# A graph attention layer: the softmax scans of both directions side by side, one feature tile per edge group

## The chip, the core and the metric

The kernel runs on one core of a Trainium2 chip. The metric is the time of one execution on the device in microseconds. Three runs of the kernel before took 5300.75, 5307.96 and 5309.53 us; their median, 5307.96 us, is the time before.

In the profile the engines are PE (TensorE's matmuls), PEld (TensorE's weight loads), DVE (VectorE), ACT (ScalarE), POOL (GpSimd) and SP (SyncE). A q behind a name is the engine's sequencer. L167 is line 167 of the kernel.

## What is computed

There are 12500 nodes with 64 features, and 400000 edges with 64 features each. The edges are sorted by their destination.

```python
h_src, h_dst = x[src], x[dst]
e = leaky_relu(concat([h_src, h_dst, edge]) @ W_attn + b_attn, 0.01)[:, 0]
m = concat([h_src, edge]) @ W_ne
ex = exp(e - segment_max(e, dst)[dst])
alpha = ex / segment_sum(ex, dst)[dst]
z = segment_sum(alpha[:, None] * m, dst)
out = relu(concat([x, z]) @ W_out)
return layernorm(x + out)
```

So each edge gets a score, a softmax runs over all edges of one destination, and the edges' features are summed with its weights. Since a destination's edges are neighbours in the list, the softmax is over runs of the list. It is made with scans along the list in both directions.

## The kernel before

A **group** is 512 edges: 128 partitions with 4 edges each. There are 782 groups. A **batch** is up to 20 groups, and its softmax is one piece of work; the batches are 4 groups, then 38 of 20, then 10 and 8. A **feature tile** is 4 groups (`SG`), so a batch of 20 has five.

`gather` (L152) fills a feature tile. It holds two arrays, `ze` with the edges' own rows and `zx` with 65 values for the edge's source node: its features and its share of the score. SyncE loads `ze` with one transfer of 512 KB (L158). GpSimd gathers `zx` with 16 indirect transfers, one per group and place (L167), from `table`, which the kernel makes itself first; the first batch gathers from `x` (`plain`), one tile of it before anything else. The pool has ten such tiles (`ZB`). A gather waits for the last product of the batch that owned the tile ten tiles earlier (L172); with five tiles to a batch this is the batch before last.

`scores` (L178) is VectorE's work per tile: a product with `w_edge` and a reduction (L190, L192), the gathered share (L197), a 0/1 array `hot` that tells which of 48 destination slots an edge belongs to (L199), the destination's share by that array (L204, L207), and the leaky ReLU (L208, L209). ScalarE copies the window of destination values `win` to PSUM (L186), from a row that SyncE loads (`wrow`, L184).

`softmax` (L252) turns a batch's scores into one long list. Its 80 groups of 128 edges (four per group) lie one per partition, 128 edges along the row (`er`, L279). A scan over the whole list is made in three steps: a scan within each partition, a scan over the 128 partial results in one row of one partition, and a second scan within the partitions from the right start. `to_row` (L212) brings the partial results into a row: a 32x32 block transpose and four copies of 32 values, each from another group of 32 partitions (L218). `to_col` (L226) goes back: four copies into `turn` (L228) and a transpose (L223). The maximum needs such a pass forwards (L283 to L293), then one backwards over its result (`total`, L295 to L306); after the exponential (L313) the sum again needs one forwards (L314 to L327) and one backwards. So four passes follow one another, and all their steps but two are VectorE's. `carry` hands the running maximum and sum to the next batch; `fac` corrects what an open run has in the accumulator already (L337 to L344).

`aggregate` (L347) makes `w`, the weights by slot, on VectorE (L350). TensorE multiplies, for each group and place, 128 edges by 48 slots: one product for the edges' own rows into partitions 0 to 63 of the result and one for the gathered rows into 64 to 127 (L358). VectorE adds each group's 48 columns to the accumulator `acc` in SBUF at a place read from memory (L368).

The main loop (L546 on) takes for each batch `gather` and `scores` tile by tile, then `softmax`, then `aggregate`. A scheduler orders the instructions of each engine from this program and its own model of time, and each engine works in that order; there is one queue per engine, and the transfers that an engine issues stand in it too. `finish1` and `finish2` (L482, L499) turn finished blocks of nodes into output, two calls at most per batch, beside the other work. `neighbours` (L231) loads the destinations with those before and behind.

## Time and profile before

| | us |
|---|---|
| median of three runs | 5307.96 |
| the profiled execution | 5279.3 |
| its span, first to last instruction | 5277.6 |
| POOL busy | 2978.4 |
| DVE busy | 2211.2 |
| PE busy | 657.6 |
| ACT busy | 245.8 |

A row of the costliest groups names line, engine, operation and tiles, then the count, the busy time in us, the mean of one in ns, and after the bar the engine's idle time just before these instructions with what ended most of it. "issue" there is time in which the engine waited for nothing that the profile shows. A row of the timeline starts with the time since the start and the duration in us, and has the idle time before it in brackets. A row of the chain of waits has start, duration, and what it was; x64 is the number of records in it.

The clock granted to TensorE was 0.57 of full speed on average: half speed, and full speed for some 7 to 14 us in each batch's products. The transfers moved 47 GB/s on average.

### The profile page before, as it was taken

The numbers are of one execution on the slowest core, as the hardware profiler recorded it, in microseconds if no ns is written. First come the engines' busy times: TensorE is split into PE (matmuls) and PEld (weight loads), VectorE is DVE, ScalarE is ACT, GpSimd is POOL, SyncE is SP. The second block draws the span as 40 slices with busy tenths as digits, with TensorE's granted clock in tenths as the row PEclk, the third lists the DMA queues.
The fourth block names the chain that finished last, engine by engine and source line by source line (L and its number), as shares of the span: only waits on it lengthen the run. The fifth ranks groups of instructions, "written<-read, shape, count | busy, mean of one in ns | idle before, by whom it ended". The sixth has DMA issues, their size and how long they took to land.

```text
span 5277.6 us, 40966 instructions
## 1 busy us (share of the span) xinstructions
PE 657.6 (12%) x13346; PEld 612.9 (12%) x13346; DVE 2211.2 (42%) x6612; ACT 245.8 (5%) x527; POOL 2978.4 (56%) x3142
## 2 busy tenths in 40 slices
PE   0010000000100111101011111111111111111113
PEld 0010000000100010101010110110111111111112
DVE  4163343344444444444444444444444444444446
ACT  0000000000000000000000000000000000000001
POOL 4745555556555555555555555555555555555550
PEclk9985555555555555555555555555555555555556
DMA  7111111122211121111111211211221222221110
GB/s 133 28 48 46 45 45 45 45 46 47 47 46 46 46 48 46 47 46 47 46 47 45 48 47 46 48 47 46 47 48 47 47 47 47 47 47 46 46 43 10
DMA packets 304921, 249.29 MB, mean 47 GB/s; under 512 B 125445, under 2 KB 253869, under 8 KB 304698
## 3 DMA queue, kind: packets, MB, share of 16 engines
q0 software_dynamic: 100320, 104.46, 10.7%
q1 hardware_dynamic: 177690, 135.46, 9.0%
q10 hardware_dynamic: 26688, 6.67, 0.6%
q8 instruction: 107, 1.75, 0.1%
q14 instruction: 116, 0.95, 0.1%
HBM read 239.69 MB, written 9.07 MB: 47 GB/s over the span
## 4 chain that ended last, share of the span: by engine, by line
issue 58%; DVE 26%; PE 7%; another core or an unknown queue 4%; DMA 2%; POOL 1%; DVEq 1%; SPq 1%; ACT 0%; ACTq 0%
PE pg L358 5%; DVE prod L190 2%; DVE hot L199 2%; DVE acc L368 2%; DVE row L218 2%; DVE turn L228 1%; DVE sdst L207 1%; DVE y L192 1%; DVE tr L215 1%; DVE prod L204 1%; POOL zx L167 1%; PE pg L505 1%; PE pg L504 1%; DMA zx<-table,srcs 1%
## 5 line engine op out<-in xcount | busy, mean ns | idle before, releaser
L167 POOL DMA_INDIRECT zx<-table,srcs x3112 | 2948.1, 947 | 2109.0 <-PE pg L358 1140.7
L358 PE MATMUL pg<-w,ze 128*64 128x48 f32 x6256 | 476.5, 249 | 3669.8 <-DVE w L350 2103.7
L358 PEld LDWEIGHTS pg<-w,ze 128*64 128x64 f32 x6256 | 468.6, 167 | 3674.9 <-DVE w L350 2007.4
L218 DVE COPY row<-tr 1x32 f32<-1x32 f32 x656 | 137.5, 210 | 847.2 <-issue 671.5
L358 PE MATMUL pg<-w,zx 128*64 128x48 f32 x6256 | 477.5, 249 | 25.7 <-issue 25.7
L358 PEld LDWEIGHTS pg<-w,zx 128*64 128x64 f32 x6256 | 468.3, 167 | 28.8 <-issue 28.8
L192 DVE TENSOR_REDUCE y<-prod 128x16 f32<-128x1024 f32 x196 | 237.4, 1211 | 3.2 <-remote 3.2
L190 DVE TENSOR_TENSOR prod<-ze,fixed 128x1024 f32<-128x1024 f32 x196 | 237.2, 1210 | 0.0
L207 DVE TENSOR_REDUCE sdst<-prod 128x16 f32<-128x768 f32 x196 | 185.4, 946 | 19.9 <-DVE drel L142 14.5
L204 DVE TENSOR_TENSOR prod<-hot,win 128x768 f32<-128x768 bf16 x196 | 186.1, 950 | 11.8 <-DVE y L197 10.7
L368 DVE TENSOR_TENSOR acc<-acc,pg 128x48 f32 x782 | 153.9, 197 | 88.3 <-PE pg L358 84.7
L199 DVE TENSOR_TENSOR hot<-fixed,drel 128x768 bf16<-128x768 f32 x196 | 185.8, 948 | 0.0
L350 DVE TENSOR_TENSOR w<-hot,fixed 128x768 f32<-128x768 bf16 x196 | 175.9, 947 | 1.2
L228 DVE COPY turn<-rt_m 1x32 f32<-1x32 f32 x164 | 34.0, 208 | 235.2 <-issue 211.1
L131 PE MATMUL pp<-ident,nat 20*128 20x20 f32 (+3 forms) x328 | 42.6, 269 | 716.3 <-DVE sdst L207 241.0
L131 PEld LDWEIGHTS pp<-ident,nat 20*128 20x128 f32 (+3 forms) x328 | 39.0, 197 | 723.4 <-issue 703.8
L186 ACT ACTIVATE win<-wrow 128x192 f32<-128x192 f32 x196 | 65.0, 331 | 1152.8 <-DVE prod L204 798.9
L134 DVE CAST srcs<-pp 128x80 int32<-128x80 f32 (+3 forms) x41 | 9.8, 238 | 249.4 <-DMA zx<-table,srcs 246.5
L228 DVE COPY turn<-top 1x32 f32<-1x32 f32 x164 | 33.6, 205 | 169.9 <-issue 168.5
L228 DVE COPY turn<-den 1x32 f32<-1x32 f32 x164 | 31.9, 194 | 157.2 <-issue 155.7
L323 ACT ACTIVATE drop<-drop 1x1 f32<-1x1 f32 x40 | 8.1, 202 | 1793.4 <-DVE b_m L306 1088.5
L505 PE MATMUL pg<-both,acc 128*128 128x64 f32 x196 | 64.4, 430 | 97.7 <-DVE acc L368 82.1
(129 smaller groups left out, 1267.9 us busy)
## 6 DMA issues: line engine op xcount, KB each, us to landing
ze<-in_edge_dram SPq DMA_DIRECT2D x194, 512.0 KB
zx<-table,srcs POOLq DMA_INDIRECT x3112
wrow<-wins SPq DMA_DIRECT2D x195, 96.0 KB
table<-xt ACTq DMA_DIRECT2D x14, 227.5 KB
xb<-in_x_dram ACTq DMA_DIRECT2D x24, 128.0 KB
out_dram<-yo SPq DMA_DIRECT2D x24, 128.0 KB
raw<-in_idx_dram SPq DMA_DIRECT2D x38, 80.0 KB
xt<-in_x_dram SPq DMA_DIRECT2D x13, 224.0 KB
```

Of the source, the lines that this page charges most:

```text
L167: got = nc.gpsimd.indirect_dma_start(out=zx[:, g, t, 0:D] if plain else zx[:, g, t, :], out_offset=None, in_=x[:, :] if plain else table[: ...
L190: nc.vector.tensor_tensor(prod[:, 0:n], ze[:, 0:n], w_edge.unsqueeze(1).to_broadcast([P, n, T, D]), op=OP.mult)
L192: nc.vector.tensor_reduce(yb, prod[:, 0:n], axis=AX.X, op=OP.add)
L199: nc.vector.tensor_tensor(hot[:, 0:n], slots.unsqueeze(1).unsqueeze(1).to_broadcast([P, n, T, S]), drel[:, :, b:b + n].rearrange("p t g -> ...
L204: nc.vector.tensor_tensor(at[:, 0:n], hot[:, 0:n], win[:, 0:n].unsqueeze(2).to_broadcast([P, n, T, S]), op=OP.mult)
L207: nc.vector.tensor_reduce(sdst[:, 0:n], at[:, 0:n], axis=AX.X, op=OP.add)
L218: nc.vector.tensor_copy(row.rearrange("o (g h) -> o h g", h=HQ)[:, h, :], tr[h * BG:h * BG + 1, :])
L228: nc.vector.tensor_copy(turn[h * BG:h * BG + 1, :], row.rearrange("o (g h) -> o h g", h=HQ)[:, h, :])
L350: nc.vector.tensor_tensor(w[:, 0:n], hot[:, 0:n], alpha[:, :, b:b + n].rearrange("p t g -> p g t").unsqueeze(3).to_broadcast([P, n, T, S]) ...
L358: last = nc.tensor.matmul(pg[at:at + D, g, :], z[:, g, t, 0:D], w[:, g, t, :], start=(t == 0), stop=(t == T - 1))
L368: added = nc.vector.tensor_tensor(ag, ag, pg[:, g, :], op=OP.add)
L505: nc.tensor.matmul(po[:, j, :], acc[:, (c0 + j) * P:(c0 + j + 1) * P], both, start=False, stop=True)
```

## The change

- The softmax's forward and backward scans no longer follow one another. Both start from the scores (later from the exponentials), lie side by side in one tile `pair`, and go through one row and back together (`to_rows`, `to_cols`). The maximum is the larger of both; the sum is both minus the edge's own value, which both hold. The correction factor of a batch's first run goes back with them as a third row of `srow`.
- A feature tile is one array `z` of 129 values per edge: 64 edge values, and the 65 gathered ones behind them. SyncE loads the edges' rows into one of two staging tiles `ze`, ScalarE copies them into `z`, and GpSimd gathers into the rest. There are nine such tiles. 
- TensorE makes one product of 128 columns per 128 edges, where it made two of 64.
- The first two batches, of 4 and 20 groups, become one of 24. All its six tiles are gathered from `x` ahead of the rest of the start.

The diff, without changed arguments of calls:

```diff
@@ -29,7 +29,9 @@
-ZB = 10
+ZB = 9
+ZW = 129
+EB = 2
@@ -151,8 +153,8 @@
     def gather(g0, n, srcs, b0, plain):
-        ze = feats.tile([P, SG, T, D], F32, name="ze")
-        zx = feats.tile([P, SG, T, EW], F32, name="zx")
+        z = feats.tile([P, SG, T, ZW], F32, name="z")
+        ze = chunks.tile([P, SG, T, D], F32, name="ze", bufs=EB)
         whole = min(n, NG - 1 - g0)
         if whole:
             nc.sync.dma_start(out=ze[:, 0:whole].rearrange("p g t f -> p g (t f)"),
@@ -161,11 +163,12 @@
             nc.vector.memset(ze[:, n - 1], 0.0)
             nc.sync.dma_start(out=ze[0:RP, n - 1],
                               in_=edge[E - REST:E, :].rearrange("(p t) f -> p t f", t=T))
+        nc.scalar.activation(z[:, 0:n, :, 0:D], ze[:, 0:n], AF.Copy)
         for g in range(n):
             for t in range(T):
                 at = srcs[:, t, g0 + g - b0:g0 + g - b0 + 1]
                 got = nc.gpsimd.indirect_dma_start(
-                    out=zx[:, g, t, 0:D] if plain else zx[:, g, t, :], out_offset=None,
+                    out=z[:, g, t, D:2 * D] if plain else z[:, g, t, D:ZW], out_offset=None,
                     in_=x[:, :] if plain else table[:, :],
                     in_offset=bass.IndirectOffsetOnAxis(ap=at, axis=0))
                 if len(owner) >= ZB:
@@ -209,24 +212,23 @@
         nc.vector.scalar_tensor_tensor(yb, sdst[:, 0:n], SLOPE, sdst[:, 0:n], op0=OP.mult, op1=OP.max)
         return hot
-    def to_row(block):
-
-        tr = rows.tile([P, BG], F32, name="tr")
-        nc.vector.transpose(tr, block)
-        row = tiny.tile([1, P], F32, name="row", bufs=1)
+    def to_rows(pair):
+
+        tr = rows.tile([P, 2, BG], F32, name="tr")
+        nc.vector.transpose(tr, pair[:, :, 0:BG])
+        row = tiny.tile([1, 2, P], F32, name="row", bufs=1)
         for h in range(HQ):
-            nc.vector.tensor_copy(row.rearrange("o (g h) -> o h g", h=HQ)[:, h, :], tr[h * BG:h * BG + 1, :])
+            nc.vector.tensor_copy(row.rearrange("o k (g h) -> o h k g", h=HQ)[:, h], tr[h * BG:h * BG + 1])
         return row
-    def turned():
-        ct = rows.tile([P, BG], F32, name="ct", bufs=2)
-        nc.vector.transpose(ct, turn)
-        return ct[:, 0:1]
-
-    def to_col(row):
+    def to_cols(row, n):
+
         for h in range(HQ):
-            nc.vector.tensor_copy(turn[h * BG:h * BG + 1, :], row.rearrange("o (g h) -> o h g", h=HQ)[:, h, :])
-        return turned()
+            nc.vector.tensor_copy(turn[h * BG:h * BG + 1, 0:n, :],
+                                  row[:, 0:n, 0:P].rearrange("o k (g h) -> o h k g", h=HQ)[:, h])
+        ct = rows.tile([P, 3, BG], F32, name="ct", bufs=2)
+        nc.vector.transpose(ct[:, 0:n, :].rearrange("r k g -> r (k g)"), turn[:, 0:n, :].rearrange("r k g -> r (k g)"))
+        return ct
     def neighbours(g0, G):
@@ -265,67 +267,81 @@
         up = tiny.tile([P, 1], F32, name="up")
         nc.vector.tensor_reduce(up, pf, axis=AX.X, op=OP.max)
         nc.vector.tensor_tensor(worst[:, 1:2], worst[:, 1:2], up, op=OP.max)
-
-        nc.vector.tensor_tensor(turn3[:, 0, 0:1], far[:, 0:1], far[:, P:P + 1], op=OP.subtract)
-        nc.vector.tensor_tensor(turn3[:, 1, 0:1], far[:, 1:2], far[:, P + 1:P + 2], op=OP.subtract)
-        nc.vector.tensor_scalar(turn3[:, 2, 0:1], turn3[:, 0, 0:1], 0.0, None, op0=OP.is_ge)
-        tr3 = rows.tile([P, 3, BG], F32, name="tr3")
-        nc.vector.transpose(tr3.rearrange("r k g -> r (k g)"), turn3.rearrange("r k g -> r (k g)"))
-        rw = tiny.tile([1, 3, P], F32, name="rw", bufs=1)
+        same_b = rows.tile([P, P], F32, name="same_b")
+        nc.vector.tensor_scalar(same_b, pb, 0.0, None, op0=OP.is_ge)
+
+        nc.vector.tensor_tensor(turn4[:, 0:2, 0], far[:, 0:2], far[:, P:P + 2], op=OP.subtract)
+        nc.vector.tensor_scalar(turn4[:, 2:4, 0], turn4[:, 0:2, 0], 0.0, None, op0=OP.is_ge)
+        tr4 = rows.tile([P, 4, BG], F32, name="tr4")
+        nc.vector.transpose(tr4.rearrange("r k g -> r (k g)"), turn4.rearrange("r k g -> r (k g)"))
+        rw = tiny.tile([1, 4, P], F32, name="rw", bufs=1)
         for h in range(HQ):
-            nc.vector.tensor_copy(rw.rearrange("o k (g h) -> o h k g", h=HQ)[:, h], tr3[h * BG:h * BG + 1])
+            nc.vector.tensor_copy(rw.rearrange("o k (g h) -> o h k g", h=HQ)[:, h], tr4[h * BG:h * BG + 1])
+
+        mrow = tiny.tile([1, 2, P + 2], F32, name="mrow")
+        srow = tiny.tile([1, 3, P + 2], F32, name="srow")
+        ROW1 = P + 1
+        flat_m = mrow.rearrange("o k i -> o (k i)")
+        flat_s = srow.rearrange("o k i -> o (k i)")
+        top, rtm = flat_m[:, 0:P + 1], flat_m[:, ROW1:ROW1 + P + 1]
+        den, rts = flat_s[:, 0:P + 1], flat_s[:, ROW1:ROW1 + P + 1]
+        nc.vector.memset(rtm[:, R:P + 1], FLOOR)
+        nc.vector.memset(rts[:, R:P + 1], 0.0)
+        if first:
+            nc.vector.memset(top[:, 0:1], FLOOR)
+            nc.vector.memset(den[:, 0:1], 0.0)
+            nc.vector.memset(srow[:, 2, 0:P], 1.0)
+        else:
+            nc.vector.tensor_copy(top[:, 0:1], carry[0])
         er = rows.tile([P, T, P // T], F32, name="er")
         nc.vector.transpose(er.rearrange("r t q -> r (t q)"), y.rearrange("p t g -> p (t g)"))
         e = rows.tile([P, P], F32, name="e")
         nc.scalar.activation(e.rearrange("r (q t) -> r q t", t=T), er.rearrange("r t q -> r q t"), AF.Copy)
-        s1 = rows.tile([P, P], F32, name="s1")
-        nc.vector.tensor_tensor_scan(s1[:, ::-1], pf, e, FLOOR, OP.add, OP.max)
-        ends = to_row(s1[:, 0:BG])
-        top = tiny.tile([1, P + 1], F32, name="top")
-        if first:
-            nc.vector.memset(top[:, 0:1], FLOOR)
-        else:
-            nc.vector.tensor_copy(top[:, 0:1], carry[0])
-        nc.vector.tensor_tensor_scan(top[:, 1:P + 1], rw[:, 0, :], ends, top[:, 0:1], OP.add, OP.max)
-        ini = to_col(top[:, 0:P])
+        pair = rows.tile([P, 2, P], F32, name="pair")
+        nc.vector.tensor_tensor_scan(pair[:, 0, ::-1], pf, e, FLOOR, OP.add, OP.max)
+        nc.vector.tensor_tensor_scan(pair[:, 1, ::-1], pb[:, ::-1], e[:, ::-1], FLOOR, OP.add, OP.max)
+        row = to_rows(pair)
+        nc.vector.tensor_tensor_scan(top[:, 1:P + 1], rw[:, 0, :], row[:, 0, :], top[:, 0:1], OP.add, OP.max)
+        nc.vector.tensor_tensor_scan(rtm[:, 0:R][:, ::-1], rw[:, 1, 0:R][:, ::-1], row[:, 1, 0:R][:, ::-1],
+                                     FLOOR, OP.add, OP.max)
+        ini = to_cols(mrow, 2)
         s2 = rows.tile([P, P], F32, name="s2")
-        nc.vector.tensor_tensor_scan(s2, pf, e, ini, OP.add, OP.max)
-
-        def total(s, name):
-
-            b1 = rows.tile([P, P], F32, name="b1")
-            nc.vector.tensor_tensor_scan(b1[:, ::-1], pb[:, ::-1], s[:, ::-1], FLOOR, OP.add, OP.max)
-            begins = to_row(b1[:, 0:BG])
-            rt = tiny.tile([1, P + 1], F32, name=f"rt_{name}")
-            nc.vector.memset(rt[:, R:P + 1], FLOOR)
-            nc.vector.tensor_tensor_scan(rt[:, 0:R][:, ::-1], rw[:, 1, 0:R][:, ::-1],
-                                         begins[:, 0:R][:, ::-1], FLOOR, OP.add, OP.max)
-            bi = to_col(rt[:, 1:P + 1])
-            b2 = rows.tile([P, P], F32, name=f"b2_{name}")
-            nc.vector.tensor_tensor_scan(b2[:, ::-1], pb[:, ::-1], s[:, ::-1], bi, OP.add, OP.max)
-            return rt, b2
-
-        rtm, mx = total(s2, "m")
+        nc.vector.tensor_tensor_scan(s2, pf, e, ini[:, 0, 0:1], OP.add, OP.max)
+        b2 = rows.tile([P, P], F32, name="b2")
+        nc.vector.tensor_tensor_scan(b2[:, ::-1], pb[:, ::-1], e[:, ::-1], ini[:, 1, 0:1], OP.add, OP.max)
         dl = rows.tile([P, P], F32, name="dl")
-        nc.vector.tensor_tensor(dl, e, mx, op=OP.subtract)
+        nc.vector.tensor_tensor(dl, s2, b2, op=OP.max)
+        nc.vector.tensor_tensor(dl, e, dl, op=OP.subtract)
         ex = rows.tile([P, P], F32, name="ex")
         nc.scalar.activation(ex, dl, AF.Exp)
-        nc.vector.tensor_tensor_scan(s1[:, ::-1], same, ex, 0.0, OP.mult, OP.add)
-        ends = to_row(s1[:, 0:BG])
-        den = tiny.tile([1, P + 1], F32, name="den")
-        if first:
-            nc.vector.memset(den[:, 0:1], 0.0)
-        else:
-            drop = tiny.tile([1, 1], F32, name="drop")
-            nc.vector.tensor_tensor(drop, top[:, 0:1], rtm[:, 0:1], op=OP.subtract)
-            nc.vector.tensor_scalar(drop, drop, 0.0, None, op0=OP.min)
-            nc.scalar.activation(drop, drop, AF.Exp)
-            nc.vector.tensor_tensor(den[:, 0:1], carry[1], drop, op=OP.mult)
-        nc.vector.tensor_tensor_scan(den[:, 1:P + 1], rw[:, 2, :], ends, den[:, 0:1], OP.mult, OP.add)
-        ini = to_col(den[:, 0:P])
-        nc.vector.tensor_tensor_scan(s2, same, ex, ini, OP.mult, OP.add)
-        rts, sm = total(s2, "s")
+        if not first:
+
+            drop = tiny.tile([1, 2], F32, name="drop")
+            nc.vector.tensor_tensor(drop[:, 0:1], top[:, 0:1], rtm[:, 0:1], op=OP.max)
+            nc.vector.tensor_tensor(drop[:, 1:2], top[:, 0:1], drop[:, 0:1], op=OP.subtract)
+            nc.scalar.activation(drop[:, 1:2], drop[:, 1:2], AF.Exp)
+            nc.vector.tensor_tensor(den[:, 0:1], carry[1], drop[:, 1:2], op=OP.mult)
+        pair = rows.tile([P, 2, P], F32, name="pair")
+        nc.vector.tensor_tensor_scan(pair[:, 0, ::-1], same, ex, 0.0, OP.mult, OP.add)
+        nc.vector.tensor_tensor_scan(pair[:, 1, ::-1], same_b[:, ::-1], ex[:, ::-1], 0.0, OP.mult, OP.add)
+        row = to_rows(pair)
+        nc.vector.tensor_tensor_scan(rts[:, 0:R][:, ::-1], rw[:, 3, 0:R][:, ::-1], row[:, 1, 0:R][:, ::-1],
+                                     0.0, OP.mult, OP.add)
+        nc.vector.tensor_tensor_scan(den[:, 1:P + 1], rw[:, 2, :], row[:, 0, :], den[:, 0:1], OP.mult, OP.add)
+        if not first:
+
+            fac1 = tiny.tile([1, 2], F32, name="fac1")
+            nc.vector.tensor_tensor(fac1[:, 0:1], rts[:, 0:1], den[:, 0:1], op=OP.add)
+            nc.vector.reciprocal(fac1[:, 1:2], fac1[:, 0:1])
+            nc.vector.tensor_scalar(srow[:, 2, 0:P], den[:, 0:1].to_broadcast([1, P]), fac1[:, 1:2], None, op0=OP.mult)
+        ini = to_cols(srow, 3)
+        nc.vector.tensor_tensor_scan(s2, same, ex, ini[:, 0, 0:1], OP.mult, OP.add)
+        sm = rows.tile([P, P], F32, name="b2")
+        nc.vector.tensor_tensor_scan(sm[:, ::-1], same_b[:, ::-1], ex[:, ::-1], ini[:, 1, 0:1], OP.mult, OP.add)
+
+        nc.vector.tensor_tensor(s2, s2, ex, op=OP.subtract)
+        nc.vector.tensor_tensor(sm, sm, s2, op=OP.add)
         nc.vector.reciprocal(sm, sm)
         al = rows.tile([P, T, P // T], F32, name="al")
         nc.vector.tensor_tensor(al.rearrange("r t q -> r q t"), ex.rearrange("r (q t) -> r q t", t=T),
@@ -335,16 +351,11 @@
         nc.scalar.activation(alpha, alpha0, AF.Copy)
         fac = None
         if not first:
-            fac1 = tiny.tile([1, 1], F32, name="fac1")
-            nc.vector.reciprocal(fac1, rts[:, 0:1])
-            nc.vector.tensor_tensor(fac1, fac1, den[:, 0:1], op=OP.mult)
-            for h in range(HQ):
-                nc.vector.tensor_copy(turn[h * BG:h * BG + 1, :], fac1.to_broadcast([1, BG]))
             fac = tiny.tile([P, 1], F32, name="fac")
-            nc.vector.tensor_copy(fac, turned())
+            nc.vector.tensor_copy(fac, ini[:, 2, 0:1])
         return fac, (top[:, R:R + 1], den[:, R:R + 1])
-    def aggregate(g0, n, ze, zx, hot, b0, fac):
+    def aggregate(g0, n, z, hot, b0, fac):
         b = g0 - b0
         w = work.tile([P, SG, T, S], F32, name="w", bufs=4)
         nc.vector.tensor_tensor(
@@ -354,9 +365,8 @@
         pg = psum.tile([P, SG, P], F32, name="pg", bufs=4)[:, :, 0:S]
         for g in range(n):
             for t in range(T):
-                for at, z in ((0, ze), (D, zx)):
-                    last = nc.tensor.matmul(pg[at:at + D, g, :], z[:, g, t, 0:D], w[:, g, t, :],
-                                     start=(t == 0), stop=(t == T - 1))
+                last = nc.tensor.matmul(pg[:, g, :], z[:, g, t, 0:2 * D], w[:, g, t, :],
+                                        start=(t == 0), stop=(t == T - 1))
         _, vs = nc.values_load_multi_w_load_instructions(
             d0i[0:1, g0:g0 + n], engines=(EngineType.DVE,), min_val=0, max_val=N - 1,
             skip_runtime_bounds_check_because=within)
@@ -377,6 +387,8 @@
     while left > 0:
         sizes.insert(0, min(left, BS))
         left -= sizes[0]
+    if sizes[0] + sizes[1] <= BG:
+        sizes[0:2] = [sizes[0] + sizes[1]]
     starts = [sum(sizes[:k]) for k in range(len(sizes))]
@@ -442,7 +454,7 @@
         zero = pre.tile([1, S], F32, name="zero", bufs=1)
         nc.vector.memset(zero, 0.0)
         nc.scalar.dma_start(out=sdflat[NB * P:NB * P + S].unsqueeze(0), in_=zero)
-        while len(ahead) < 5 and (len(ahead) + 1) * SG <= sizes[0]:
+        while len(ahead) < 6 and (len(ahead) + 1) * SG <= sizes[0]:
             ahead.append(gather(len(ahead) * SG, SG, prepared[0][0], 0, True))
         NW = (NG + P - 1) // P
         d0p = pre.tile([P, NW], I32, name="d0p", bufs=1)
```

## The prediction

> **What bounds the kernel now.** I read the page first, for who waits for whom.
>
> ```profile
> span 5277.6 us, 40966 instructions
> ...
> PE 657.6 (12%) x13346; PEld 612.9 (12%) x13346; DVE 2211.2 (42%) x6612; ACT 245.8 (5%) x527; POOL 2978.4 (56%) x3142
> ...
> L167 POOL DMA_INDIRECT zx<-table,srcs x3112 | 2948.1, 947 | 2109.0 <-PE pg L358 1140.7
> ...
> L218 DVE COPY row<-tr 1x32 f32<-1x32 f32 x656 | 137.5, 210 | 847.2 <-issue 671.5
> ```
>
> No engine is full. GpSimd, which issues the gathers, loses 1140.7 us to TensorE's edge products, which free the feature tiles. The 210 ns row copies of the softmax have six times their own length of idle time in front of them. So I looked at GpSimd's order of time around one such wait:
>
> ```profile
> 2267.68 0.95 POOL L167 DMA_INDIRECT zx<-table,srcs  x1 [0.31 <-issue]
> 2297.46 0.95 POOL L167 DMA_INDIRECT zx<-table,srcs  x1 [28.83 <-PE pg L358]
> 2298.71 0.95 POOL L167 DMA_INDIRECT zx<-table,srcs  x1 [0.30 <-issue]
> ```
>
> A gather takes 1.25 us from start to start, so the 80 of a batch of 20 groups take 100 us; then GpSimd stands for 28.8 us until the batch before last is summed. What VectorE does meanwhile, in one softmax while gathers run, and in the last softmax (8 groups), when all gathers are over:
>
> ```profile
> 2206.58 0.18 DVE L218 COPY row<-tr 1x32 f32<-1x32 f32 x1 [0.50 <-DVE tr L215]
> 2208.65 0.18 DVE L218 COPY row<-tr 1x32 f32<-1x32 f32 x1 [1.88 <-issue]
> 2210.05 0.18 DVE L218 COPY row<-tr 1x32 f32<-1x32 f32 x1 [1.22 <-issue]
> 2211.46 0.19 DVE L218 COPY row<-tr 1x32 f32<-1x32 f32 x1 [1.23 <-issue]
> 2212.85 0.47 DVE L290 TENSOR_TENSOR_SCAN top<-rw,top,row 1x128 f32<-1x128 f32 x1 [1.20 <-issue]
> ```
> ```profile
> 5232.57 0.31 DVE L279 STREAM_TRANSPOSE er<-y 128x128 f32<-128x128 f32 x1
> ...
> 5233.83 0.21 DVE L215 STREAM_TRANSPOSE tr<-s 128x32 f32<-128x32 f32 x1
> 5234.08 0.78 DVE L218 COPY row<-tr 1x32 f32<-1x32 f32 x4
> 5234.89 0.47 DVE L290 TENSOR_TENSOR_SCAN top<-rw,top,row 1x128 f32<-1x128 f32 x1
> ...
> 5251.30 1.81 DVE L350 TENSOR_TENSOR w<-hot,fixed 128x768 f32<-128x768 bf16 x2
> ```
>
> The same four copies take 0.78 us in the second fence, and 1.4 to 2.1 us each in the first. The whole softmax, from er (L279) to the first w (L350), is 18.7 us at the end, but 83.9 us (2200.97 to 2284.87) in mid-run. I call these **slow steps**. In the order of time they begin about 20 us after a row of gathers begins (2449 after 2428) and last until about 8 us after it ends (2276.5 after 2268.6). Long scoring instructions hide them; a chain of short ones pays for each.
>
> So VectorE's chain sets the period: from one w to the next, 6 us of w and first sums, 29 us of scores, 84 of softmax. GpSimd restarts at 478.0 (when batches 0 to 2, 44 groups, are summed) and, 35 periods on, at 5052.1: **130.7 us a period**. 478 + 36 x 130.7 + 95 for the last two batches gives the span.
>
> **The change, part by part.**
>
> Softmax. Taken from 2200.97 on, it now has four passes through one row: 20.5, 21.7, 18.6 and 11.5 us (the last half fast), 5.9 us for subtraction and exp after the second, 3.8 us of tail. Each pass has a scan, a transpose, 4 row copies, a row scan, 4 turn copies, a transpose and a scan. The change keeps passes one and three, makes them double width, and drops two and four. Per pass the second column scan, row scan and grown scan lie beside the first ones and add 0.35 + 0.45 + 0.5 = 1.3 us (start to start of neighbouring independent scans, as L298 to L260: 0.34). First half: 1.9 + 20.5 + 1.3, then max 2.8 (a waited step after a scan was 1.4 to 4.2), subtraction 1.4, exp 1.7: 29.6. Second half: 18.6 + 1.3, the batch factor's add, reciprocal and product now in front of the turn copies 3.5, then six slow steps to alpha with one 0.95 us reciprocal 9.8: 33.2. The four rw copies lay in the fast tail; now they meet slow steps, 4 x 1.4 = 5.6. Together **68 us** (57 if fillers hide, 75 if max, thresholds and memsets pay too), against 84.
>
> Feature tiles, 9 for 10. A gather waits for the last product of the batch that owned the tile nine before. The fifth tile of a batch now depends on the batch just before, not on the one before that. So a new loop: last product of batch k, 16 gathers of the fifth tile of k+1 (0.3 + 15 x 1.25 + 0.95 = 20.0), landing 2.3 (after 2267.68 the DMA share is zero by 2270.0), L197, L208, L209 and er at slow steps 5.2: er at **27.5**. Then softmax 68, and w to last product 12.6 (2284.87 to 2297.46): 108.1. Queued behind the fifth tile on GpSimd are the four first tiles of k+2, 80 us, which end at 100, in time. In batches that also finish output blocks (25 blocks, in every second batch or so) er came 32 to 34 us after the restart and w to last product took 15.3: 33.5 + 68 + 15.3 = 116.8. The mean, **112.5 us**, is the new period. GpSimd idles 12 us in it, barely more than the 8 us after which slow steps end.
>
> Edge rows. 196 copies of 128x1024 by ScalarE, near its row for 20x1024 (1056 ns): 5.3 us a period on an engine 5% busy, hidden by the gathers. Moved with it: the edge load waits for the copy two before, not for a tile; on SyncE's queue the wrow, d and raw loads stand behind it, on ScalarE's win, e, exp and alpha behind the copy. A load landed in 6 to 9 us in the chain, and scoring a tile takes 5.8. I take 0; without cover it is up to 7 us a tile. If the interleaved tile makes L190 wait for the gathers too, er is later by some 7 us in plain batches, 100 to 160 us in all; I leave that to the range.
>
> One product for two. The rows nearest in the chain:
>
> ```profile
> 2194.78 1.03 PE pp L131 x8
> ...
> 2285.92 3.67 PE pg L358 x64
> ```
>
> 64 records (32 pairs) in 3.67 us, less 0.34 for the last, are 0.107 us a pair: two loads of 64 columns at half clock. Eight transposes that each load 128 columns take 1.03 us with 0.27 of drain: 0.11. So a full-width load hides the matmul before it and costs what the pair did: **0**. Here a rule speaks against the change: the Trainium skill, "TensorE: Matmul & The Clock Gate", Part 3, what overlaps and what doesn't, says a weight load overlaps a running matmul only where the row groups differ. These have one row group. By it, 48 columns more at the page's 1.2 GHz, 0.15 a record cold and 0.075 warm, give some 2.4 us a batch, 90 in all. I take the row; the upper end is the pace of L504 and L505 in the last microseconds (0.36 warm, 0.6 cold per product of two records): +17 us a batch.
>
> A second rule, for the slow steps: "SBUF — State Buffer", Who interferes with whom, has VectorE's two-port copies and two-input instructions blocked while a GpSimd instruction holds the shared port. By it a copy would wait at most for one gather, 0.95 + 0.18 = 1.1 us, and be fast once GpSimd stops. The row has 1.4, and 2.8 us steps after the stop (2270.97, 2273.77, 2276.54). At 1.1 the softmax is 54 us and GpSimd's 100 us would bound: 4116. I take the row.
>
> Start. 96 gathers now come from x without waiting for the table. Before: 16 of them until 32.9, then GpSimd stood until 76.5. Now 32.9 + 80 x 1.25 = 133 to 135, the seven window gathers to 144, three tiles of batch 1 to 204. Scores of 24 groups end near 175, the softmax is slow until 212, then fast: summed near 238. Two tiles 40, er 7.5, 68, 12.6: **366** for the 44 groups that took 478. End: two short batches after the last long one, 95 less two dropped passes, 88.
>
> **Sum:** 366 + 36 x 112.5 + 88 = 4504 us of span. The profiled run was 5279.3, 1.7 over its span; the median of the runs, 5307.96, is 0.54% over that: **4530 us**.
>
> **Rivals.**
> - GpSimd bounds: softmax under 58, period 100 to 101: 366 + 36 x 101 + 88 = 4090, as run 4115. For: 80 x 1.25 leaves nothing below; against: 68 needs every filler hidden.
> - Slow steps reach the scores: if GpSimd idles under 8 us they never end, and five tiles pay some 3.5 us each: a period of 122 to 126, 4870 to 5020. For: 12 us is close to 8; against: longer periods bring idle time back.
> - Slower: ScalarE's queue. A copy whose edge load is late stands before the win copy of a tile being scored. Fully exposed it is 7 us a tile, 35 a batch: period 147.5, 5790. It decides from 4.3 us a tile (a period of 134.0 gives 5308). For: two staging tiles; against: two loads in flight halve 6 to 9 us to less than the 5.8 of a tile.
> - No gain, because the chain dropped was covered: against it, the 28.8 us wait ends on that chain. It would give 5300.
>
> **How the numbers follow.** The forecast 0.61 (4310 to 4780 for a softmax of 62 to 75), GpSimd 0.09, slow scores 0.16, ScalarE 0.12, no gain 0.02. The range of 4170 to 5030 leaves out GpSimd's end and the slower case. Faster 0.86, same 0.02, slower 0.12; within 0.2% a measurement can't tell it from no change.
>
> **What would show it.** GpSimd's gaps of 30 us shrink to about 12, in front of the fifth tile's gathers; restarts 105 to 120 apart; er to w 62 to 75 us; copies of 2x32 still 1.4 us apart; the products of a batch still 12 to 15 us; 96 gathers in one row at the start. Wrong if ScalarE's win waits for edge loads, or slow steps appear in all five tiles.

## The result, and the profile after

The changed kernel took **5901.15 us** (median of 4 runs, 5900.91 to 5905.64), the kernel before beside it 5304.97 (4 runs): a ratio of **1.113, 95% interval 1.111 to 1.115**. The forecast was 4530. It is slower by 596 us, and 1371 us from the forecast.

One thing has to be known for all that follows. The kernels were run on several chips, which fall into two kinds. On those called **chip A** here, the kernel before takes 5286 to 5308 us and VectorE has the slow steps of the prediction. Three of them are the numbers 0, 14 and 15; that of the result is not known by its number, but its times are of this kind. On **chip B**, number 6, which was used in one session, the same kernel takes 4234 us, and the traces taken there have no slow steps. The kernel before was measured beside every run; runs from different chips A are compared by their ratios to it. Where nothing is said, it is chip A. The changed kernel took 5882.48 and 5901.89 us when it was measured again on chip 0 (ratios 1.113 and 1.112).

The page of the changed kernel, the rows that answer those shown of before:

```profile
span 5899.2 us, 28738 instructions
...
PE 1538.0 (26%) x7082; PEld 1490.1 (25%) x7082; DVE 2121.0 (36%) x5695; ACT 439.1 (7%) x718; POOL 2971.4 (50%) x3142
...
L170 POOL DMA_INDIRECT z<-table,srcs x3032 | 2867.9, 946 | 2789.1 <-issue 2768.7
L368 PE MATMUL pg<-w,z 128*128 128x48 f32 x6256 | 1349.1, 413 | 3238.5 <-DVE w L361 3238.5
...
L221 DVE COPY row<-tr 1x64 f32<-1x64 f32 x320 | 79.5, 249 | 535.1 <-issue 441.3
```

The records on TensorE are nearly halved, 7082 for 13346, and its busy time is more than doubled, 1538.0 for 657.6 us. GpSimd's idle time in front of gathers has risen from 2109.0 to 2789.1 us. GpSimd's order of time around one of its waits, where before had 28.83 us:

```profile
2312.09 0.94 POOL L170 DMA_INDIRECT z<-table,srcs  x1 [0.30 <-issue]
2360.69 0.94 POOL L170 DMA_INDIRECT z<-table,srcs  x1 [47.65 <-issue]
2361.93 0.94 POOL L170 DMA_INDIRECT z<-table,srcs  x1 [0.30 <-issue]
```

The gap is 47.65 us, and there is one in each batch. What fills it is in the chain of waits over the same time (start, length, what, number of records):

```profile
2324.80 27.54 PE pg L368 x128
2352.34 0.62 PE pg L516 x2
2352.95 7.00 PE pg L368 x32
```

A tile has 32 records, two for each product, and takes 6.9 us, where before had 64 records in 3.67. From the first to the last record a batch of 20 groups takes 34.7 us (median over the batches); before, it was 13.8. A record starts every 0.213 us, without a change over the whole run. The profile of the changed kernel holds no record of the clock granted to TensorE (its mean is listed as 1.00 for want of one); what the pace says of the clock is worked out below.

VectorE in the second half of the same softmax, and the same copies in the last softmax, with no gathers beside it:

```profile
2282.09 0.21 DVE L221 COPY row<-tr 1x64 f32<-1x64 f32 x1 [2.50 <-remote]
2288.35 0.29 DVE L221 COPY row<-tr 1x64 f32<-1x64 f32 x1 [6.05 <-issue]
2290.45 0.21 DVE L221 COPY row<-tr 1x64 f32<-1x64 f32 x1 [1.81 <-issue]
...
2298.85 0.27 DVE L279 COPY rw<-tr 1x128 f32<-1x128 f32 x1 [4.02 <-issue]
```
```profile
5853.23 0.89 DVE L221 COPY row<-tr 1x64 f32<-1x64 f32 x4
```

The slow steps are still there. From er to the first w it is 82.8 us (median over the batches), against 85.3 before and 68 forecast. So the forecast's gain in the softmax is missing, and TensorE has added 21 us to each batch.

### The profile page after: what moved, and what is told of

Same layout as the page of the kernel before. It is cut to its first block, busy times and chain, and to the rows that moved or that the text cites. A ratio compares the mean times of both kernels' runs of the same rounds, so it can differ in the third digit from the quotient of the medians.

```text
span 5899.2 us, 28738 instructions
## 1 busy us (share of the span) xinstructions
PE 1538.0 (26%) x7082; PEld 1490.1 (25%) x7082; DVE 2121.0 (36%) x5695; ACT 439.1 (7%) x718; POOL 2971.4 (50%) x3142
## 4 chain that ended last, share of the span: by engine, by line
issue 35%; DVE 25%; PE 22%; another core or an unknown queue 13%; POOL 3%; DMA 1%; ACT 1%; DVEq 0%; SPq 0%; ACTq 0%; POOLq 0%
PE pg L368 21%; POOL z L170 3%; DVE turn L227 1%; DVE sdst L210 1%; DVE row L221 1%; DVE prod L193 1%; DVE rw L279 1%; DVE prod L207 1%; DVE hot L202 1%; DVE y L195 1%; DVE tr L218 1%; DMA z<-table,srcs 1%; DVE w L361 1%; DVE b L345 1%
## 5 line engine op out<-in xcount | busy, mean ns | idle before, releaser
L170 POOL DMA_INDIRECT z<-table,srcs x3032 | 2867.9, 946 | 2789.1 <-issue 2768.7
L368 PE MATMUL pg<-w,z 128*128 128x48 f32 x6256 | 1349.1, 413 | 3238.5 <-DVE w L361 3238.5
L368 PEld LDWEIGHTS pg<-w,z 128*128 128x128 f32 x6256 | 1339.2, 333 | 3246.1 <-DVE w L361 3243.5
L166 ACT ACTIVATE z<-ze 128x1024 f32<-128x1024 f32 x196 | 208.2, 1062 | 1241.9 <-PE pg L368 1176.6
L221 DVE COPY row<-tr 1x64 f32<-1x64 f32 x320 | 79.5, 249 | 535.1 <-issue 441.3
L193 DVE TENSOR_TENSOR prod<-z,fixed 128x1024 f32<-128x1024 f32 x196 | 237.3, 1211 | 0.0
L279 DVE COPY rw<-tr 1x128 f32<-1x128 f32 x160 | 47.6, 298 | 244.9 <-issue 226.3
L227 DVE COPY turn<-mrow 1x64 f32<-1x64 f32 x160 | 37.0, 232 | 245.7 <-issue 226.7
L170 POOL DMA_INDIRECT z<-in_x_dram,srcs x96 | 96.1, 1001 | 33.5 <-issue 28.7
L227 DVE COPY turn<-srow 1x96 f32<-1x96 f32 x160 | 49.7, 311 | 160.5 <-issue 160.3
L517 PE MATMUL pg<-both,acc 128*128 128x64 f32 x196 | 66.9, 446 | 38.4 <-DVE acc L378 38.4
## 6 DMA issues: line engine op xcount, KB each, us to landing
xt<-in_x_dram SPq DMA_DIRECT2D x13, 224.0 KB
```

The lines of the kernel that those rows point to most:

```text
L166: nc.scalar.activation(z[:, 0:n, :, 0:D], ze[:, 0:n], AF.Copy)
L170: got = nc.gpsimd.indirect_dma_start(out=z[:, g, t, D:2 * D] if plain else z[:, g, t, D:ZW], out_offset=None, in_=x[:, :] if plain else ta ...
L193: nc.vector.tensor_tensor(prod[:, 0:n], z[:, 0:n, :, 0:D], w_edge.unsqueeze(1).to_broadcast([P, n, T, D]), op=OP.mult)
L221: nc.vector.tensor_copy(row.rearrange("o k (g h) -> o h k g", h=HQ)[:, h], tr[h * BG:h * BG + 1])
L227: nc.vector.tensor_copy(turn[h * BG:h * BG + 1, 0:n, :], row[:, 0:n, 0:P].rearrange("o k (g h) -> o h k g", h=HQ)[:, h])
L368: last = nc.tensor.matmul(pg[:, g, :], z[:, g, t, 0:2 * D], w[:, g, t, :], start=(t == 0), stop=(t == T - 1))
```

## Experiments

### Which part costs the time: products, softmax, copies

Four kernels each take back one part of the change, or have one part alone.

`a`, two products of 64 columns again, from the interleaved tile:

```
-                last = nc.tensor.matmul(pg[:, g, :], z[:, g, t, 0:2 * D], w[:, g, t, :],
-                                        start=(t == 0), stop=(t == T - 1))
+                for at in (0, D):
+                    last = nc.tensor.matmul(pg[at:at + D, g, :], z[:, g, t, at:at + D], w[:, g, t, :],
+                                            start=(t == 0), stop=(t == T - 1))
```

> The changed kernel with one edit: each 128 edges again get two products of 64 columns (both halves of the same interleaved tile) in place of one of 128. Theory 'product': a product of 128 columns costs two records of 0.213 us, one after the other, where the two products of 64 columns cost 0.12 to 0.21 together; the 20 groups of a batch take 34 us on TensorE instead of 12.6, every microsecond of it stands in the cycle from one release of the feature tiles to the next. Then the period falls from 148.5 to about 127 us, 38 batches, and the time is 5030 to 5150. Theory 'ScalarE queue': the copies of edge rows, which stand ahead of the win copies, hold the period; the products are not what counts, the period stays above 143 and the time above 5700.

`c`, the changed kernel with the softmax of before, four passes (`softmax`, `to_row`, `to_col`, `turned`) in place of the two:

> The changed kernel with the softmax of before (four passes, one after the other) put back, all else as changed. Theory 'window': while gathers run every short VectorE step is slow until some 8 us after the last gather; in both kernels the first w comes 10 to 16 us after the last gather of the row, so the length of the chain hardly counts; the old softmax loses only its fast end, w comes 3 to 6 us later in a batch, 38 batches: 6000 to 6130. Theory 'chain': the two passes dropped were worth the forecast 16 us a batch; then 16 x 38 is lost, 6400 to 6550.

`d`, the kernel before with the new `softmax`, `to_rows` and `to_cols` and nothing else:

> The kernel before with the new softmax alone (ten pairs of separate tiles, two products, first batch short). Theory 'window': er comes 32 us after GpSimd restarts, the gathers last 100 us and slow steps 108; w came 117 us after the restart and comes now at 110 to 114: 3 to 7 us a batch are gained, 38 batches, 5040 to 5200. Theory 'chain' (the forecast's step, softmax 84 to 68 us): 16 a batch, 4650 to 4750. Theory 'no gain': within 10 us of the kernel before.

`f`, as `a`, and the edge rows loaded straight into a tile of their own:

```
-        z = feats.tile([P, SG, T, ZW], F32, name="z")
-        ze = chunks.tile([P, SG, T, D], F32, name="ze", bufs=EB)
+        ze = feats.tile([P, SG, T, D], F32, name="ze")
+        zx = feats.tile([P, SG, T, EW], F32, name="zx")
...
-        nc.scalar.activation(z[:, 0:n, :, 0:D], ze[:, 0:n], AF.Copy)
```

> As the run with two products, and the edge rows are again loaded straight into a tile of their own, no copy by ScalarE; nine pairs of tiles as in the changed kernel. Theory 'product': the copy was hidden but for the fifth tile's, which starts when the batch before is summed; against the run with two products 0 to 2.5 us a batch, 0 to 95 us, so 4950 to 5130. Theory 'ScalarE queue': the copies hold the win copies up by 5 us or more a batch: over 190 us less than the run with two products.

These ran on chip B: the kernel before took 4234.46 us there, and no expectation speaks of that case. `a` took 4016.56 (ratio 0.949, 0.947 to 0.951), `c` 4087.23 (0.965, 0.964 to 0.967), `d` 4331.55 (1.023, 1.021 to 1.025), `f` 4016.47 (0.949). So the times can't be held against the expectations, but the traces explain what chip B lacks. One softmax of `a` there, from er (L298) over four copies of the second half to the first w, and a gather of the same microseconds:

```profile
1974.88 0.31 DVE L298 STREAM_TRANSPOSE er<-y 128x128 f32<-128x128 f32 x1
...
1983.27 0.96 DVE L221 COPY row<-tr 1x64 f32<-1x64 f32 x4
...
1992.06 3.55 DVE L361 TENSOR_TENSOR w<-hot,fixed 128x768 f32<-128x768 bf16 x4 [0.35 <-ACT fixed L351]
```
```profile
1983.98 0.94 POOL L170 DMA_INDIRECT z<-table,srcs  x1 [0.31 <-issue]
```

The same instructions take 17.2 us with gathers going on beside them, and GpSimd never stops after the start: 2984 gathers in one row from 224.0 to 3960.2 us. There a batch lasts the 100 us of its gathers. `c` gathers without a gap as well, from 256.9 us on: there even the 34.7 us of the single product fit beside the gathers, and that kernel is 3.5% under the kernel before.

`d` is slower than the kernel before on chip B. Its trace shows a wait that costs it time. VectorE's order after the softmax's product al:

```profile
1814.52 0.38 DVE L344 TENSOR_TENSOR al<-ex,b 128x128 f32<-128x128 f32 x1
1875.18 0.24 DVE L134 CAST srcs<-pp 128x80 int32<-128x80 f32 x1 [60.29 <-DMA zx<-table,srcs]
1875.34 0.30 DVE L347 STREAM_TRANSPOSE alpha<-al 128x128 f32<-128x128 f32 x1
```

The index cast of a later batch stands in VectorE's queue in front of the softmax's last transpose and waits until the row of gathers has landed. All products of the batch wait behind it, and after them GpSimd, for 23 us in each of the first 15 batches; then gathers catch up and run without a gap. No trace of the kernel before on chip B was kept, so it is not shown that this wait is what sets the two apart.

### Whose are the slow steps

> The changed kernel, unaltered, measured beside the kernel before on one chip again, because the kernel before took 4234 us beside the first four experiments and 5305 beside the changed kernel, and in the trace of the run with two products no VectorE step is slow while gathers run. Theory 'slow steps are not the kernel's': where the kernel before takes some 4234 us, the changed kernel has no slow steps either, its softmax takes 17 to 20 us, GpSimd gathers without a gap after the start and the time is 4000 to 4100, 3 to 6 per cent under the kernel before. Theory 'slow steps are the kernel's': the changed kernel has them again and takes 5850 to 5950, whatever the kernel before takes.

It took 5882.48 us, the kernel before 5286.30 (ratio 1.113, 1.111 to 1.115): this was chip A. Where the kernel before takes some 5290 us, the changed kernel has its slow steps too; so whether they are the kernel's alone isn't decided by this run. It is decided by `a`, whose next run was on chip A.

### The parts again, on chip A

> The changed kernel with two products of 64 columns for each 128 edges, again, to have it where VectorE has slow steps (the kernel before at some 5290 us) if this chip has them. Theory 'product in the cycle': w comes some 111 us after GpSimd restarts whatever the products cost, since slow steps last until 8 us after the last gather; the products of a batch take 12 to 15 us in place of 34; the period is 124 to 128 and the time 4980 to 5150, under the kernel before. Theory 'the 34 us are hidden': above 5700. Where the kernel before takes 4234 us: 4017 again.

> The kernel before with the new softmax alone, again, for the same reason. Where the kernel before takes some 5290 us. Theory 'window': w comes 110 to 114 us after the restart instead of 117, products as before: 5040 to 5200. Theory 'chain' (the forecast's 84 to 68 us): 4650 to 4750. Where the kernel before takes 4234 us: 4331 again, for there VectorE stands in front of L134, which waits for the last gather of the row.

`e` is the rest of the change without the interleaved tile: the kernel before with the new softmax and the first batch of 24 groups.

> The kernel before with the new softmax and a first batch of 24 groups: ten pairs of separate tiles, two products, no copy by ScalarE; what is left of the change when the interleaved tile is taken out. Where the kernel before takes some 5290 us: the run with the new softmax alone less what the longer first batch gives, 40 to 110 us. Where it takes 4234 us: if L134 stands in front of the last softmax step as in the run with the new softmax alone, the period is 123 us and the time some 4250; if GpSimd never stops, as with nine pairs, 4000 to 4050.

> The changed kernel beside these three on the same chip. Where the kernel before takes some 5290 us: 5870 to 5910 again. Where it takes 4234 us: theory 'slow steps are not the kernel's': its softmax takes 17 to 20 us, the 34 us of a batch's products are hidden behind 100 us of gathers, GpSimd sets the end: 4000 to 4100. Theory 'products bound': 34 us of products on the way to the release of the tiles keep GpSimd waiting even then, over 4300.

All four ran on chip 0, beside the same runs of the kernel before (5307.56 us):

| kernel | us | ratio to before (95%) | what it adds to the row above |
|---|---|---|---|
| new softmax (`d2`) | 5175.11 | 0.975 (0.973 to 0.976) | -132 us: the softmax |
| and first batch of 24 (`e`) | 5106.84 | 0.962 (0.960 to 0.964) | -68 us: the start |
| and interleaved tile, copy, nine tiles (`a2`) | 5095.84 | 0.960 (0.959 to 0.962) | -11 us: copy and tiles (the intervals overlap) |
| and one product (the changed kernel) | 5901.89 | 1.112 (1.110 to 1.113) | **+806 us: the product** |

The single edit from the third row to the fourth is worth more than all the loss. A tile's records in the chain of waits of `a2`, and GpSimd's wait in that batch:

```profile
2658.49 3.56 PE pg L369 x64
```
```profile
2642.05 0.94 POOL L170 DMA_INDIRECT z<-table,srcs  x1 [0.30 <-issue]
2670.25 0.94 POOL L170 DMA_INDIRECT z<-table,srcs  x1 [27.25 <-issue]
```

3.56 us for a tile instead of 6.9, and a batch takes 13.8 us on TensorE instead of 34.7. The 20.9 us come off GpSimd's wait: its 38 waits sum to 1876.7 us in the changed kernel and to 1092.0 in `a2`, which is 785 of the 806. The time is inside the 4980 to 5150 of "product in the cycle". `a` took 4017 us on chip B and 5096 here, with the same instructions in the same order, and er to w is 17.2 us there and 82.6 here. So the slow steps don't come from the kernel alone. They go with the chip, or with the session: chip B was one chip in one session, and no run tells the two apart. For `d2`, "window" was right, 5175 of 5040 to 5200 (w comes 114 us after the restart, 116 before), and "chain", the forecast's step, wrong by at least 425 us.

The old softmax in the changed kernel, on chip A:

> The changed kernel with the softmax of before, again, for a chip whose VectorE has slow steps. Where the kernel before takes some 5300 us: by what the new softmax alone gave there (132 us), 6000 to 6100; by the forecast's 16 us a batch, 6400 to 6550. Where it takes 4234 us: 4087 again.

6017.29 us, beside 5288.54 of the kernel before: a ratio of 1.138 (1.136 to 1.140), against 1.112 with the new softmax. The difference of 0.026 is 138 us, near the 132 of `d2`: the softmax is worth the same with either product.

### What a product of 128 columns is made of

`g` is `e` with the order of the products changed: four of one half, then four of the other.

```
             for t in range(T):
-                for at, z in ((0, ze), (D, zx)):
+            for at, z in ((0, ze), (D, zx)):
+                for t in range(T):
```

> The run with ten pairs of tiles, two products of 64 columns, with nothing but the order of the products changed: for each group first the four products of the edge rows, all into the first half of the columns, then the four of the gathered rows, all into the second half, where the two halves took turns before. Theory 'halves side by side': the weight load of one column half runs beside the work of the other half; a record of 64 columns takes 0.107 us alone (half of the 0.213 of 128 columns) and two halves in turn give 0.053; in the new order most neighbours are in one half, 128 edges take 0.35 to 0.43 us instead of 0.21 or less, the products of a batch 26 to 34 us. Where the kernel before takes some 5290 us: 5107 plus 38 times 13 to 21, 5600 to 5900. Where it takes 4234 us the products may be hidden, and the records decide. Theory 'width': a load of 64 columns is short by itself, whichever half: 12 to 15 us a batch as before, 5107 within 30.

5132.76 us on chip 15 (ratio 0.968, 0.967 to 0.970), 26 us over `e`, or 33 by the ratios. On the time, "width" is about right. But TensorE did not keep to the program's order:

```profile
2436.23 0.74 PE L368 MATMUL pg<-w,ze 128*64 128x48 f32 x5 [87.47 <-issue]
2436.66 0.34 PE L368 MATMUL pg<-w,zx 128*64 128x48 f32 x1
2436.77 0.31 PE L368 MATMUL pg<-w,ze 128*64 128x48 f32 x1
2436.81 0.31 PE L368 MATMUL pg<-w,zx 128*64 128x48 f32 x1
```

After five records of one half, in the middle of its third product, those of the other begin in between, mostly 0.107 us apart within each half at first. So this run could not put the halves one after the other, and does not separate the two theories.

`j` is the changed kernel with half of the columns streamed: `pg[:, g, 0:S // 2]` and `w[:, g, t, 0:S // 2]`. The other half of the sums is left out.

> The changed kernel, with only 24 of the 48 columns of w streamed through each product of 128 columns, and only those added; the sums of slots 24 to 47 are left out. Theory 'load': a record takes the time of loading 128 columns and hides its stream; records stay 0.213 us apart, a batch's products 34 us, the time within 60 us of the changed kernel on the same chip (5902 where the kernel before takes 5290). Theory 'load and stream in turn': a record falls to 0.17 to 0.19 us, the batch to 27 to 31 us, the time by 110 to 270 us.

5913.71 us, a ratio of 1.115 (1.113 to 1.117), where the changed kernel has 1.112 (1.110 to 1.113) on chip 0. Its row on the page:

```profile
L368 PE MATMUL pg<-w,z 128*128 128x24 f32 x6256 | 1346.7, 388 | 3265.8 <-DVE w L361 3265.8
```

Records stay 0.213 us apart, a batch 34.7 us. Between 24 and 48 columns the stream costs nothing: theory "load".

`k` is `e` with the products of the gathered rows left out:

```
-                for at, z in ((0, ze), (D, zx)):
+                for at, z in ((0, ze),):
...
-            ag = acc[:, ds(vs[g], S)]
-            added = nc.vector.tensor_tensor(ag, ag, pg[:, g, :], op=OP.add)
+            ag = acc[0:D, ds(vs[g], S)]
+            added = nc.vector.tensor_tensor(ag, ag, pg[0:D, g, :], op=OP.add)
```

> The run with ten pairs of tiles and two products, with the second product left out (the gathered rows are not summed; only the half of the sums that comes from the edge rows is added). Theory 'halves side by side': the two products of 128 edges ran at the same time, one in each half of the columns; one alone takes as long as both did: its records stay 0.107 us apart at half clock, 160 records are 17 us, 9 to 12 us if the clock rises; the time is within -40 and +190 of the run with both (5107 where the kernel before takes 5300). Theory 'in turn': the records of the two halves followed each other 0.053 us apart, one half alone needs half the time, 5 to 8 us a batch, and the time falls by 100 to 190 us. On the clock: if it rises only where both halves work, the records stay 0.107 apart through the whole batch, as those of 128 columns stay 0.213; if any steady work lifts it, they fall to 0.053 after some microseconds.

5104.62 us, beside 5288.54 of the kernel before (ratio 0.966, 0.964 to 0.967; `e` 0.962, 0.960 to 0.964). First one batch of `e`, in the chain of waits, then one of `k`, in the order of time:

```profile
2677.99 11.62 PE pg L368 x320
```
```profile
2671.89 11.64 PE L368 MATMUL pg<-w,ze 128*64 128x48 f32 x160 [90.80 <-DVE w L360]
```

Half the records take the same time. The two products of 64 columns **run side by side**, one in each half of the columns, and the second is free. In `k` the records are 0.107 us apart at first and 0.059 after some microseconds. The clock granted in these 15 us is 0.81 on average, and 0.83 in 15 us around the batch of `e`. Over the run, all but two of the 4006 short steps fall where full speed is granted, and none of the 2081 long ones. So the clock rises with one half alone; "only where both halves work" is wrong.

### A version that goes further

`h` is `e` with the twenty small copies of a softmax moved to ScalarE, in `to_rows`, `to_cols` and for `rw`:

```
-            nc.vector.tensor_copy(row.rearrange("o k (g h) -> o h k g", h=HQ)[:, h], tr[h * BG:h * BG + 1])
+            nc.scalar.activation(row.rearrange("o k (g h) -> o h k g", h=HQ)[:, h], tr[h * BG:h * BG + 1], AF.Copy)
```

> The run with ten pairs of tiles and two products, with the twenty small copies of a softmax (row, turn and rw) moved from VectorE to ScalarE. Where the kernel before takes some 5290 us (slow steps). Theory 'VectorE only': ScalarE's copies take 0.2 to 0.35 us each even while gathers run; of some 55 slow steps 35 stay, er to w falls from 84 to 50 to 65 us, w comes 85 to 97 us after the restart, the period is 100 to 111 us and the time 4150 to 4550. Theory 'all engines': ScalarE's copies come 1.4 us apart as well, 5050 to 5200. Theory 'window': w can't come before 8 us after the last gather, 5000 to 5107. Where the kernel before takes 4234 us: 4000 to 4100 or 4250, as the order of L134 falls.

**4953.41 us, a ratio of 0.934 (0.933 to 0.936)**: it beats the kernel before and every other version on chip A, but it lies in no theory's range, 403 us over the top of "VectorE only" and 47 under "window". er to w fell to 64.7 us (median), near that theory's upper end. In one batch, ScalarE's four copies, VectorE's w, then TensorE's records and GpSimd's last gather and restart:

```profile
2440.66 1.29 ACT L220 ACTIVATE row<-tr 1x64 f32<-1x64 f32 x4 [12.35 <-issue]
...
2467.51 3.55 DVE L360 TENSOR_TENSOR w<-hot,fixed 128x768 f32<-128x768 bf16 x4 [1.40 <-issue]
```
```profile
2472.18 0.31 PE L368 MATMUL pg<-w,ze 128*64 128x48 f32 x1
2474.19 0.24 PE L368 MATMUL pg<-w,ze 128*64 128x48 f32 x1 [1.70 <-issue]
2476.99 0.24 PE L368 MATMUL pg<-w,zx 128*64 128x48 f32 x1 [2.57 <-issue]
```
```profile
2478.85 0.94 POOL L169 DMA_INDIRECT zx<-table,srcs  x1 [0.30 <-issue]
2504.07 0.94 POOL L169 DMA_INDIRECT zx<-table,srcs  x1 [24.28 <-PE pg L368]
```

Four copies take 1.29 us on ScalarE in the middle of the gathers. The first w comes 12 us before the last gather ends, so "window" is no law for w. But then TensorE has slow steps itself: 41 records from 2470.01 to 2472.18, then single ones 1.4 to 2.8 us apart until 2492.38, 12.6 us after the last gather, though no semaphore holds them. Over the batches, w comes 17 us earlier after the restart than in `e` (means, 96.4 for 113.2), and the products take 11 us longer (24.4 for 13.0). So most of what was gained on VectorE is lost on TensorE.

## Why the prediction was wrong, step by step

**The step that failed: "one product for two", put at 0.** It measured +806 us, 20.9 us a batch. The sum took a record of 128 columns at 0.11 us, from eight transposes, and set it against 0.107 us for "a pair" of records with 64. Two things were wrong in that. A product's record of 128 columns takes 0.213 us: a transpose, which has one record where a product has two, was no measure for it. And the 0.107 us of a pair was read as two loads one after the other, but it is the time of one record (`k`), while one of the other half runs beside it. The trace of before had this in plain sight, in TensorE's order of time:

```profile
2285.92 0.31 PE L358 MATMUL pg<-w,ze 128*64 128x48 f32 x1 [90.11 <-issue]
2285.93 0.34 PE L358 MATMUL pg<-w,zx 128*64 128x48 f32 x1
2286.03 0.31 PE L358 MATMUL pg<-w,ze 128*64 128x48 f32 x1
2286.07 0.31 PE L358 MATMUL pg<-w,zx 128*64 128x48 f32 x1
```

So 128 edges cost 2 x 0.107 = 0.21 us at the lower clock with two products, and 2 x 0.213 = 0.43 with one. That is a factor of two. The rest is the clock: with records of 64 columns it rises within a batch (0.107 to 0.059 us), with 128 columns the pace did not change in 34.7 us without a pause. That the clock stayed low is worked out from other products, for the six runs with products of 128 columns have no clock record at all, while each of the ten with 64 has 40 to 50 grants of full speed. L504 and L505 of before multiply the same shapes as L516 and L517 of the changed kernel. In before, records of these come 0.27 us apart outside those grants and 0.16 apart inside, 41 times; none of the six runs has one of the short kind.

The rule that spoke against the change (the Trainium skill, "TensorE: Matmul & The Clock Gate", Part 3, what overlaps and what doesn't) pointed the right way, and I took the row against it. But the estimate made from it, 2.4 us a batch, let the stream add to the load, and it comes out with 80 records in a batch, where there are 160. In these runs the load alone sets the pace: `j` halves the stream and nothing changes. And loads do overlap, between column halves with the same rows, which that rule leaves out (`e` and `k`). The upper end of my bounds, +17 us a batch from L504 and L505, was nearly what it took, in part by luck, for it was their pace at the higher clock; with it the sum would have been 4504 + 36 x 17 = 5116.

**Softmax, 84 to 68 us: wrong.** Worth 132 us where 16 x 36 = 576 were put. The first half was right: 29.6 us forecast from er to the exp, 29.8 measured. The second half took 53 for 33.2. The sum counted dropped passes as slow steps. In a batch of before (median) 55 VectorE instructions lie between er and 8 us after the last gather and take 77 us; 26 more follow in 8.2 us. In `d2` it is 55 in 79 us and 13 in 6.8. The change drops 14 instructions, and 13 of them come off the fast end: the chain moves forward, but into the slow time come as many others, the next batch's thresholds, masks and rw copies among them (18 instructions and 20 us in the softmax shown above).

**Period of 112.5 us: wrong also where its softmax is right.** `h` has er to w at 64.7, below the 68, and its period is 123 to 124: "w to last product 12.6" holds only after the gathers. When w came earlier, TensorE had slow steps of its own.

**Fifth tile behind the batch just before, er at 27.5: right.** Measured 28.6 us after GpSimd's restart at 2213.3. **Edge copies at 0: right.** Copies, interleaving and nine tiles together are -11 us on chip A, hardly clear of noise, and the copy with its tile is 0.1 us on chip B (`a` against `f`). The rival "ScalarE's queue" ends at 5790, near the result, by another mechanism: the copies do wait for TensorE, 1176.6 us in all, but where the products are short nothing is lost by it (`a2`). **Start: half right.** 68 us for 112; GpSimd restarted after 44 groups at 395 us in `a2`, where 366 was forecast, and at 442 in the changed kernel, with 34.7 us of products.

Adding up: the forecast had 778 us of gain, the parts give 132 + 68 + 11 = 211, which is 567 missing, and the product 806: together 1373, against the 1371 us by which the forecast missed. The parts were taken one on top of the other, in the table's order.

**What stays open.** Why chip A has slow steps and chip B none. They are not VectorE's alone (TensorE in `h`), and the shared port is not enough: by "SBUF — State Buffer", Who interferes with whom, they would be on chip B too, where four copies take 0.96 us between gathers 1.25 apart. Late code is an unlikely cause, though not excluded: the 16 KB code packets of queue q8 take about 1 us on both chips, and none of them starts between 2380 and 2493 in the batch of `h` shown, so nine slow records in a row don't each wait for one. Open too is why loads of 128 columns never raise the clock. The changed kernel itself was not measured on chip B; from `c` it may well be faster than the kernel before there, so the loss of 11% is a result of chip A.

## What to carry to other kernels

Price an operation by a row of its own kind: the same number of records, the same columns loaded, the same neighbours on the array; then look at which records lie side by side before two are made into one. Where a chain runs through a slow stretch that ends at its own time, taking instructions out of the chain saves the price of the last ones, not the mean. Measure a kernel that lives on overlap on more than one chip, and compare only within one.

## What the runs showed of the hardware

- f32 products with 48 columns streamed: a record that loads 128 columns takes 0.213 us, with 24 columns streamed too (`j`); one of 64 columns takes 0.107, and 0.059 at the higher clock (`k`). "TensorE: Matmul & The Clock Gate", LDWEIGHTS, has the time of a load go by its columns; an estimate by its formula at the lower clock is 107 ns for 128. The proportion agrees, the amount is twice that here.
- Products of 64 columns into the two halves of the columns run at the same time: 320 records in 11.62 us, 160 of one half in 11.64, and TensorE brings them side by side even where the program has them four by four (`g`).
- 34.7 us of back-to-back products of 128 columns did not raise TensorE's clock: none of the six runs with them has a clock record, and in none do the records of L504 and L505 (there under other numbers) come 0.16 us apart. The same page's Part 1 has it rise after some 3.4 us of sustained activity. Products of 64 columns raised it 40 to 50 times a run.
- The same kernel on chip B and on chips A: 4234 and 5286 to 5308 us. In `a`, er to w is 17.2 and 82.6 us, by steps of VectorE that come 0.2 to 0.3 us apart on one and often 1.4 to 2.8 us on the other while GpSimd gathers. ScalarE's four copies took 1.29 us in the same stretch (`h`).
